# The last layer's attention in float32r halves, with its transfers merged and GpSimd's work tied to the program's order

## The chip, the cores and the metric

The kernel runs on one core of a Trainium2 chip. TensorE (PE) multiplies matrices and writes to PSUM; VectorE (DVE), ScalarE (ACT) and GpSimd (POOL) work element by element; SyncE (SP) issues the transfers, which 16 DMA engines carry out. The engines run side by side, each through its own instructions in order, and wait for each other by semaphores. The metric is device time in microseconds (us) of one execution; a time stands for the median of several.

## The reference, cut to what matters

Four layers run one after another over a state x of 4 sequences of 1024 tokens and 128 channels. The change is in the last one: attention with relative positions in 16 heads of 8 channels, times the silu of a gated feed-forward whose weights are stored as whole numbers.

```python
qx = split_head(x @ Wq.T); kx = split_head(x @ Wk.T); vx = split_head(x @ Wv.T)
ex = rel_embed[ns].reshape(n, NH, HD).transpose(1, 0, 2)
srel = srel_skew(jnp.einsum('bhnd,hmd->bhnm', qx, ex))
qk = (jnp.einsum('bhnd,bhmd->bhnm', qx, kx) + srel) * inv_dim
mask = 1000000000.0 * jnp.triu(jnp.ones((n, n), dtype=x.dtype), 1)
atten = jax.nn.softmax(qk - mask, axis=-1)
out = jnp.einsum('bhnm,bhmd->bhnd', atten, vx)   # heads joined again
s = out @ Wp.T + bp
# feed-forward, weights times 1/127
g = silu((silu(x @ wg.T) * (x @ wu.T)) @ wd.T)
x = x + s * g                                    # q, k, v and g from layernorm(x)
```

The table rel_embed has 256 rows, so distances repeat: srel_skew turns a row of 256 products per query into values by key.

## The kernel before, in words

Python code writes out every instruction; a framework then orders each engine's list by its own estimate of when operands are ready, places the tiles in memory and adds the semaphores. So the order on an engine follows the order of the code only roughly, unless an instruction is pinned with `keep_in_program_order`, which puts it behind everything written before it for its engine.

**Units.** The last layer (`layer3`, L1725) goes through 4 sequences, 4 groups i of four heads in each, and 8 tiles t of 128 queries in the order `ORDER3` = 7, 0, 6, 1, 5, 2, 4, 3: 128 units. Four heads lie at rows 0, 32, 64 and 96 of a 128-row tile, each with its 8 channels in the first 8 of its 32 rows; the other 24 rows are zero, set once (L1745). So one head's product takes 32 rows of TensorE's array, and four heads sit in it at once.

**Scores** (`scores3`, L2048). Per unit, in steps of up to 512 keys: four products of k and q into one PSUM tile of four banks, of which there is one (`"sc": 1`), L2068; then on DVE, head by head, the part beyond four tiles back (L2076) and the rest with its distances added (L2083), both with the running minimum; after the last step ACT takes the exponential (L2090). The exponentials are transposed on DVE (L1797) and weigh the values on PE (`weigh3`, L2104), two tiles of queries at a time. `finish3` (L2112) divides at the end of a group, `end3` (L2128) joins the heads at the end of a sequence and stores.

**Distances** (`relative3`, L1992). Products of q with the embeddings `emb` (L2004) for two heads and two tiles, two PSUM tiles of the three tagged "tr", copied by ACT (L2006) and written to DRAM in four transfers (L2009, L2010): 256 columns and the first 128 again, for either tile. Eight such parts belong to a group; the loop runs seven parts ahead. `shear3` (L2013) reads them back with a row step one element short, which does the skew (L2025, L2027, L2031), and GpSimd masks them (L2035). `ahead(n + 3)` calls it for the unit three further on, into two buffers for tiles 4 to 7 and one for tiles 0 to 3.

**Beside that**, one step per unit: `ffn3` (L1942) in each sequence's second group (gate and up products L1953, silu and copy on ACT L1957 and L1958, their product h on GpSimd L1959, down product L1963); `begin3` (L1903) in the third group for the next sequence: layernorm, then q and k stored to DRAM (L1927) and v (L1939). The first sequence's are made by `begin_first` (L1864) during the end of the third layer, and the weights by `prepare3` (L1676). `project3` (L1968) loads the next group's q and k, four heads' 8 rows in a transfer each (L1975); `values3` (L1979) loads v four times in pieces of 32 numbers (L1985) and copies it on GpSimd into the layout of the weighing (L1989).

The order of the work around the change is set by the loop at the end of `layer3`: per step of 512 keys the next products, a transpose, some weighing, the comparison; per unit the loads and steps named above. `step` and the lists `weighs` and `transposes` keep a unit's transposes one step behind its comparison. SP's queue carries all transfers in one order.

Of the kernel before, what the change touches and what calls it, by code (L numbers as in the profile page):

```python
# [12 lines left out]
I32 = mybir.dt.int32  # L13
AF = mybir.ActivationFunctionType
# [15 lines left out]
def _constants():  # L30
# [20 lines left out]

    parts.append(("rep8", np.where(row < 8, (col % 8) == row, 0.0)))
# [1623 lines left out]
def prepare3(k, w, W, ps):  # L1676
# [21 lines left out]
    W["emb"] = new("emb", [P, 4, 256])  # L1698
    with k.tc.tile_pool(name="pad3", bufs=1) as rp:
        pad = rp.tile([P, 2, 512], F32, tag="pad", name="pad")  # L1700
        nc.vector.memset(pad, 0.0)
        for c in range(2):
            for i in range(4):
                nc.gpsimd.tensor_copy(spread(pad[:, c, :])[:, i], heads_of(W["rel"][:, c, :])[:, i])
        for i in range(4):
            k.transpose_tiles(ps, "tr", [pad[:, c, i * P : (i + 1) * P] for c in (0, 1)], W["emb"][:, i, :])
            yield

        e0 = rp.tile([P, 4], F32, tag="e0", name="e0")
        nc.vector.tensor_copy(e0, W["emb"][:, :, 0])  # L1710
        for i in range(4):
            nc.vector.tensor_scalar(W["emb"][:, i, :], W["emb"][:, i, :], e0[:, i : i + 1], None, op0=ALU.subtract)
        nc.vector.tensor_scalar(W["emb"][:, :, 0], e0, -1.0, None, op0=ALU.mult)
        for name in ("gate", "up", "down"):
            f = rp.tile([P, 3, D], F32, tag="f" + name, name="f" + name)
# [9 lines left out]
def layer3(k, W, x3, out, eps5, ps, first):  # L1725
# [12 lines left out]
    with ExitStack() as st:  # L1738
# [3 lines left out]
        for n in range(2):  # L1742
            q, kk = p1.tile([P, 1 + T], F32, tag=f"q{n}", name="q"), p1.tile([P, T], F32, tag=f"k{n}", name="k")
            for a in (q, kk):
                (nc.gpsimd if n else nc.vector).memset(a, 0.0)  # L1745
            pairs.append((q, kk))
# [5 lines left out]
        def part(h):  # L1752

            at, h = divmod(h, 8)
            if at < 4 * NB:
                pair = ORDER3[h // 4 * 4 + h // 2 % 2] // 2
                if h % 2 == 0:
                    flats[at, pair] = dram.tile([2, 4, P, 384], F32, tag="flat", name="flat")
# [70 lines left out]
        for x, (n, first) in enumerate(tiles + [(len(units), 0)] * 4):  # L1829
# [25 lines left out]
            if pos == 6 and at + 1 < 4 * NB:  # L1855
                values = values3(k, p1, batch[(at + 1) // 4], vb, (at + 1) % 4)
                next(values)
            next(beside, None)
            ahead(n + 3)
        while weighs:  # L1860
            step()


def begin_first(k, W, pool, ps, x, eps5, first):  # L1864
# [9 lines left out]
    for n, name in enumerate(("WqT", "WkT")):  # L1874
# [6 lines left out]
        nc.sync.dma_start(out=first["qk"][n], in_=qk)  # L1881
        yield
    v = pool.tile([P, NT, D], F32, tag="ret", name="v")
    for half in range(2):
# [4 lines left out]
        nc.scalar.copy(v[:, 4 * half : 4 * half + 4], pv)  # L1889
    nc.sync.dma_start(out=first["vd"].rearrange("(t p) d -> p t d", p=P), in_=v)  # L1890
# [12 lines left out]
def begin3(k, W, p1, p2, temp, ps, dram, x3, b, eps5, seq):  # L1903
# [15 lines left out]
    seq["qk"] = dram.tile([2, P, T], F32, tag="qk", name="qk")  # L1919
    for n, name in enumerate(("WqT", "WkT")):  # L1920
# [6 lines left out]
        nc.sync.dma_start(out=seq["qk"][n], in_=qk)  # L1927
        yield
    v = temp.tile([P, NT, D], F32, tag="temp", name="v")
    for half in range(2):  # L1930
# [4 lines left out]
        nc.scalar.copy(v[:, 4 * half : 4 * half + 4], pv)  # L1935
        if half == 0:
            yield
    seq["vd"] = vd = dram.tile([T, D], F32, tag="vd", name="vd")
    nc.sync.dma_start(out=vd.rearrange("(t p) d -> p t d", p=P), in_=v)  # L1939


def ffn3(k, W, p1, temp, ps, seq):  # L1942
# [3 lines left out]
    for half in range(2):  # L1946
        tok = seq["xnT"][:, half * 512 : (half + 1) * 512].rearrange("p (t a i) -> p a t i", t=4, a=4)
        for first in (0, 2):
            h, up = (temp.tile([P, 3, 256], F32, tag="temp", name=name) for name in ("h", "up"))
            for c in range(3):  # L1950
# [8 lines left out]
                nc.gpsimd.tensor_tensor(h[:, c, :], h[:, c, :], up[:, c, :], ALU.mult)  # L1959
# [8 lines left out]
def project3(k, p2, pairs, seq, i, group):  # L1968

    nc = k.nc  # L1970
    q, kk = pairs
    group.update({"q": q, "k": kk, "sums": p2.tile([P, 4, NT], F32, tag="sums", name="sums")})
    for n, dst in ((0, q[:, 1:]), (1, kk)):
        for j in range(4):
            nc.sync.dma_start(out=dst[32 * j : 32 * j + 8], in_=seq["qk"][n, 32 * i + 8 * j : 32 * i + 8 * j + 8])  # L1975
# [3 lines left out]
def values3(k, p1, seq, vb, i):  # L1979
# [3 lines left out]
    for a in range(4):  # L1983
        rows = slice(32 * a, 32 * a + 32)
        nc.sync.dma_start(out=v[rows], in_=seq["vd"].rearrange("(n r) d -> r n d", r=32)[:, :, 32 * i : 32 * i + 32])  # L1985
    yield
    for a in range(4):
        rows = slice(32 * a, 32 * a + 32)
        nc.gpsimd.tensor_copy(vb[rows, :, :, a, :], v[rows].rearrange("p n (j d) -> p n j d", d=8))  # L1989


def relative3(k, W, temp, ps, flat, q, i, pair, jp):  # L1992
# [14 lines left out]
    rows = flat.rearrange("m j p u -> p j m u")  # L2007
    for m in range(2):
# [223 lines left out]
```

## Time and profile before

| what | us |
|---|---|
| median of 3 runs (3195.61 to 3202.51) | 3196.14 |
| the profiled execution | 3191.88 |
| its span, first to last instruction | 3190.2 |
| last layer: first loads, first score, last group's end | 2143, 2155, 3168 |
| DVE, PE, ACT, POOL busy from 2155 to 3168 | 809, 807, 632, 290 |
| share of the 16 DMA engines there | 0.70 |
| TensorE's mean granted clock there | 0.76 |

The page gives each engine's busy time, then the span in 40 slices with the busy share in tenths. A group line reads: line of the code, engine, operation, tiles written and read, shape, count, then busy time in us, mean ns of one, and the idle time of the engine ahead of it with what ended it. A line of waits reads: who waited for whom, us in all, how often, the longest. A line of the view by stretches reads: from and to, length, then busy us of PE, its weight loads, DVE, ACT and POOL with counts, granted clock, share of the DMA engines, GB/s.

The last layer's 16 groups end where the sums are inverted (L2115). Their lengths in us are, in order: 69.3, 72.5, 60.2, 64.4; 61.6, 69.6, 60.2, 58.8; 60.3, 71.1, 60.4, 60.7; 62.4, 68.9, 56.9, 55.5. The second of each four has the feed-forward beside it. "Plain" below are the third and fourth of the first three sequences, the first of the second to fourth, and the third of the last. 22.4 us follow the last group.

### The profile page before, as it was taken

To read this page: it belongs to the slowest core of one execution; us is meant where nothing else is said; L and a number is where in the kernel's file an instruction comes from. 1 tells how busy PE (TensorE), PEld (TensorE's weight loads), DVE (VectorE), ACT (ScalarE), POOL (GpSimd) and SP (SyncE) were. 2 spreads that over 40 slices of the span, in tenths; PEclk is the share of its full clock that TensorE was granted. 3 is DMA by queue.
4 is the path that set the end of the run, shared out by engine and by line. 5 is a ranking of instruction groups with operands and counts; after the bars stand their busy time and mean duration, and the time that the engine had idled before them with its cause. 6 is when DMAs were issued, how large, how long until landed. Compare 5 with 4: busy or idle time off the path is not lost. (4 is left out here: it accounts for less than half of the span.)

```text
span 3190.2 us, 50621 instructions
## 1 busy us (share of the span) xinstructions
PE 2246.5 (70%) x18321; PEld 1278.9 (40%) x18321; DVE 2302.6 (72%) x5540; ACT 1494.7 (47%) x3256; POOL 1155.6 (36%) x1086
## 2 busy tenths in 40 slices
PE   5787778577787776894443674367877877878875
PEld 2555556232333332561110222244544544545553
DVE  5555544878888886657777888656788788788786
ACT  3554544333333333525332463136665765665663
POOL 3433444144444444223477433232322322323322
PEclk9888888588878877895655566566877877877776
DMA  3000000100000000320333446328677677677772
GB/s 81 13 1 1 1 1 1 35 0 0 0 0 7 6 1 7 114 98 20 73 106 112 128 107 145 101 90 252 179 217 213 191 215 230 185 221 203 209 233 65
DMA packets 397311, 308.18 MB, mean 97 GB/s; under 512 B 96369, under 2 KB 379885, under 8 KB 391429
## 3 DMA queue, kind: packets, MB, share of 16 engines
q1 hardware_dynamic: 395908, 300.75, 32.9%
q10 hardware_dynamic: 1152, 4.19, 0.4%
q8 instruction: 144, 2.36, 0.3%
q14 instruction: 107, 0.87, 0.1%
HBM read 162.72 MB, written 141.56 MB: 95 GB/s over the span
## 5 line engine op out<-in xcount | busy, mean ns | idle before, releaser
L2090 ACT ACTIVATE neg<-neg,low 128x640 f32<-128x640 f32 (+7 forms) x512 | 390.1, 763 | 168.4 <-DVE low L2083 168.1
L2035 POOL TENSOR_SCALAR_AFFINE_SELECT rel<-rel 128x512 f32<-128x512 f32 x288 | 180.2, 637 | 625.6 <-DMA rel<-flat 459.6
L1797 DVE STREAM_TRANSPOSE wT<-neg 128x640 f32<-128x640 f32 (+7 forms) x512 | 361.7, 754 | 15.8 <-ACT neg L2090 13.4
L2068 PE MATMUL score<-k,q 32*128 32x512 f32 (+3 forms) x1536 | 276.5, 702 | 103.1 <-DVE low L2083 102.5
L2083 DVE CUSTOM_DVE_ANT_0 neg<-score,rel,low 128x128 f32<-128x128 f32 (+3 forms) x448 | 217.3, 517 | 138.2 <-issue 67.2
L2004 PE MATMUL pr<-emb,q 32*128 32x256 f32 x1024 | 227.5, 525 | 62.2 <-ACT r L2006 37.1
L2104 PE MATMUL po<-wT,vb 128*32 128x64 f32 (+1 forms) x10240 | 216.6, 241 | 44.4 <-issue 30.8
L2104 PEld LDWEIGHTS po<-wT,vb 128*32 128x32 f32 x10240 | 184.3, 128 | 144.1 <-issue 85.2
L2004 PEld LDWEIGHTS pr<-emb,q 32*128 32x128 f32 x1024 | 146.1, 249 | 136.9 <-ACT r L2006 69.1
L2006 ACT COPY r<-pr 128x512 f32<-128x512 f32 x256 | 136.4, 581 | 128.8 <-PE pr L2004 95.3
L2068 PEld LDWEIGHTS score<-k,q 32*128 32x128 f32 x1536 | 98.5, 236 | 159.8 <-DVE low L2083 115.5
L2083 DVE CUSTOM_DVE_ANT_0 neg<-score,rel 128x512 f32<-128x512 f32 (+3 forms) x320 | 149.2, 521 | 18.4 <-PE score L2068 7.2
L835 PE MATMUL pg<-xnT,w 128*128 128x512 f32 x256 | 148.1, 662 | 6.7 <-DVE h L839 3.1
L788 POOL TENSOR_TENSOR prod<-rest,kv 128x2048 f32<-128x2048 f32 x32 | 145.2, 4571 | 18.4 <-ACT rest L778 18.4
L837 PE MATMUL pu<-xin,w 128*128 128x512 f32 x256 | 141.2, 635 | 13.7 <-DVE h L839 7.6
L826 PE MATMUL po<-h,w 128*128 128x512 f32 x256 | 131.4, 635 | 26.9 <-DVE h L839 26.9
L838 ACT ACTIVATE h<-pg 128x512 f32<-128x512 f32 x128 | 75.9, 595 | 156.8 <-PE pg L835 156.7
L214 PE MATMUL pt<-ident,three 128*24 128x128 bf16 x64 | 9.2, 295 | 197.5 <-DVE three L211 197.5
L1084 PE MATMUL ph<-xin,upT 128*128 128x512 bf16 (+1 forms) x128 | 69.7, 574 | 65.2 <-DVE xin L1078 63.8
L431 PE MATMUL px<-hT,xbcT 128*128 128x512 f32 x256 | 114.7, 592 | 0.0
L1489 PE MATMUL read<-kt,const_sb 128*128 128x128 f32 x256 | 50.7, 370 | 90.3 <-POOL kt L1484 90.3
L783 DVE TENSOR_REDUCE s<-prod 128x128 f32<-128x2048 f32 x32 | 73.1, 2284 | 49.4 <-POOL prod L788 49.4
(634 smaller groups left out, 5662.8 us busy)
## 6 DMA issues: line engine op xcount, KB each, us to landing
flat<-r SPq DMA_DIRECT2D x256, 256.0 KB
rel<-flat SPq DMA_DIRECT2D x112, 512.0 KB
flat<-r SPq DMA_DIRECT2D x256, 128.0 KB
rel<-flat SPq DMA_DIRECT2D x96, 256.0 KB
kt<-kd SPq DMA_DIRECT2D x16, 512.0 KB
qt<-qd SPq DMA_DIRECT2D x16, 512.0 KB
kdc<-kdd SPq DMA_DIRECT2D x16, 512.0 KB
ktc<-ktd SPq DMA_DIRECT2D x16, 512.0 KB
```

The costliest lines, as they stand in the source:

```text
L788: nc.gpsimd.tensor_tensor(prod, attn.rearrange("p (t h g) -> p t h g", t=4, g=16)[:, t].unsqueeze(2).to_broadcast(each), kv[:, t, 1, :].re ...
L826: nc.tensor.matmul(po, W["w2"][:, e, c, :], h[:, c, :], start=(e == 0 and c == 0), stop=(e == 7 and c == 1))
L835: nc.tensor.matmul(pg, W["w1"][:, e, c * P : (c + 1) * P], xnT, start=True, stop=True)
L837: nc.tensor.matmul(pu, W["w3"][:, e, c * P : (c + 1) * P], xin, start=True, stop=True)
L1797: nc.vector.transpose(weights[at, pair][j][:, t % 2, 0 : (t + 1) * P], S[j][:, 0 : (t + 1) * P])
L2004: nc.tensor.matmul(to[:, m, :], q[at, t * P : (t + 1) * P], W["emb"][at, i, :], start=True, stop=True)
L2006: nc.scalar.copy(r[:, n], to)
L2035: nc.gpsimd.affine_select(out=rel[:, :, slot(back), :], in_=rel[:, :, slot(0), :], compare_op=op, fill=fill, base=0, pattern=[[0, 4], [-si ...
L2068: nc.tensor.matmul(sc[:, j, 0 : last - first], q[at(j), 1 + t * P : 1 + n], kk[at(j), first:last], start=True, stop=True)
L2083: nc.vector.tensor_tensor_reduce(out=neg[:, begin:last], in0=sc[:, j, begin - first : last - first], in1=rel[:, j, slot : slot + (last - b ...
L2090: nc.scalar.activation(neg[:, 0:n], neg[:, 0:n], AF.Exp, bias=here, scale=-1.0, accum_out=group["sums"][:, j, t : t + 1])
L2104: nc.tensor.matmul(o[32 * j : 32 * j + 32, 2 * pair + m.start : 2 * pair + 2, :], vb[:, kb, j].rearrange("p a d -> p (a d)"), weights[j][: ...
```

## The change

q and k become float32r tiles. Each number is split into a rounded half and the rest, and the 32 rows of a head hold four copies of its 8 channels: rounded, rounded, rest, rest for q, and rounded, rest, rounded, rest for k and the embeddings. The product over 32 rows is the sum of all four cross products. Each tensor in DRAM gets the shape in which it is read, so that q, k and v of a group come in one transfer each, and the distances of two tiles are written by two transfers in place of four. Three kinds of GpSimd work are pinned to the order of the code. The loads of distances are called for ahead of the step beside the unit.

```diff
@@ prepare3
+    W["emb"] = w.tile([P, 4, 256], F32R, tag="emb", name="emb")
...
-        nc.vector.memset(pad, 0.0)
+            for r in range(4):
+                nc.gpsimd.tensor_copy(
+                    pad[:, c, :].rearrange("p (n r d) -> p n r d", r=4, d=8)[:, :, r], W["rel"][:, c, :].rearrange("p (n d) -> p n d", d=8)
+                )
...
+            nc.vector.tensor_copy(e0, emb[:, 0:1])
+            nc.vector.tensor_scalar(emb, emb, e0, None, op0=ALU.subtract)
+            nc.vector.tensor_scalar(emb[:, 0:1], e0, -1.0, None, op0=ALU.mult)
+            nc.scalar.copy(high, emb)
+            nc.vector.tensor_tensor(emb, emb, high.bitcast(F32), ALU.subtract)
+            nc.vector.tensor_scalar(emb, emb, low, None, op0=ALU.mult)
+            nc.vector.scalar_tensor_tensor(W["emb"][:, i, :], high.bitcast(F32), top, emb, op0=ALU.mult, op1=ALU.add)
@@ layer3
-            q, kk = p1.tile([P, 1 + T], F32, tag=f"q{n}", name="q"), p1.tile([P, T], F32, tag=f"k{n}", name="k")
-            for a in (q, kk):
-                (nc.gpsimd if n else nc.vector).memset(a, 0.0)
+            q, kk = p1.tile([P, 1 + T], F32R, tag=f"q{n}", name="q"), p1.tile([P, T], F32R, tag=f"k{n}", name="k")
+            nc.vector.memset(q[:, 0:1].bitcast(F32), 0.0)
...
+            ahead(n + 3)
             next(beside, None)
-            ahead(n + 3)
@@ new, called by begin_first (by halves of 512 tokens) and begin3
+def halves3(k, n, high, a, to):
+    nc = k.nc
+    rows = to.rearrange("i j (h d) t -> h (i j) d t", h=4)
+    nc.scalar.copy(high, a)
+    for h in (0, 1 + n):
+        nc.sync.dma_start(out=rows[h], in_=high.bitcast(F32))
+    k.tc.keep_in_program_order(nc.gpsimd.tensor_tensor(a, a, high.bitcast(F32), ALU.subtract))
+    for h in (2 - n, 3):
+        nc.sync.dma_start(out=rows[h], in_=a)
+def keep_values3(nc, to, v):
+    for a in range(4):
+        nc.sync.dma_start(out=to[:, :, a], in_=v[32 * a : 32 * a + 32])
@@ begin3
-        nc.sync.dma_start(out=seq["qk"][n], in_=qk)
+        halves3(k, n, temp.tile([P, T], F32R, tag="temp", name="high"), qk, seq["qk"][n])
@@ ffn3
-                nc.gpsimd.tensor_tensor(h[:, c, :], h[:, c, :], up[:, c, :], ALU.mult)
+                k.tc.keep_in_program_order(nc.gpsimd.tensor_tensor(h[:, c, :], h[:, c, :], up[:, c, :], ALU.mult))
@@ project3
-        for j in range(4):
-            nc.sync.dma_start(out=dst[32 * j : 32 * j + 8], in_=seq["qk"][n, 32 * i + 8 * j : 32 * i + 8 * j + 8])
+        nc.sync.dma_start(out=dst.bitcast(F32), in_=seq["qk"][n, i].rearrange("j r t -> (j r) t"))
@@ values3
-    for a in range(4):
-        rows = slice(32 * a, 32 * a + 32)
-        nc.sync.dma_start(out=v[rows], in_=seq["vd"].rearrange("(n r) d -> r n d", r=32)[:, :, 32 * i : 32 * i + 32])
+    nc.sync.dma_start(out=v.rearrange("p n d -> p (n d)"), in_=bass.AP(at.tensor, at.offset, [(0, 4), (4096, 32), (1, 1024)]))
...
-        nc.gpsimd.tensor_copy(vb[rows, :, :, a, :], v[rows].rearrange("p n (j d) -> p n j d", d=8))
+        k.tc.keep_in_program_order(nc.gpsimd.tensor_copy(vb[rows, :, :, a, :], v[rows].rearrange("p n (j d) -> p n j d", d=8)))
@@ relative3, with flat of [P, 4, 2, 384] in place of [2, 4, P, 384]
-    for m in range(2):
-        nc.sync.dma_start(out=rows[:, 2 * jp : 2 * jp + 2, m, 0:256], in_=r[:, :, m])
-        nc.sync.dma_start(out=rows[:, 2 * jp : 2 * jp + 2, m, 256:384], in_=r[:, :, m, 0:P])
+    nc.sync.dma_start(out=rows[:, :, 0:256], in_=r)
+    nc.sync.dma_start(out=rows[:, :, 256:384], in_=r[:, :, 0:P])
@@ shear3
-    shear = lambda n: bass.AP(base.tensor, base.offset + t % 2 * 4 * P * 384 + P, [(383, P), (P * 384, 4), (1, n)])
+    shear = lambda n: bass.AP(base.tensor, base.offset + t % 2 * 384 + P, [(8 * 384 - 1, P), (768, 4), (1, n)])
@@ end3
-    k.update(x, s, seq["g"])
+    k.tc.keep_in_program_order(nc.gpsimd.tensor_tensor(s, s, seq["g"], ALU.mult))
+    k.tc.keep_in_program_order(nc.gpsimd.tensor_tensor(x, x, s, ALU.add))
```

## The prediction

> **What bounds the kernel now.** I first read the page's slices, to see which stage the change touches. The last layer starts at 2143 us, which is slice 27 of 40.
>
> ```profile
> PE   5787778577787776894443674367877877878875
> DVE  5555544878888886657777888656788788788786
> PEclk9888888588878877895655566566877877877776
> DMA  3000000100000000320333446328677677677772
> ```
>
> The reader is to see that no engine stands at 9 there: VectorE (DVE) and TensorE (PE) share the stage at 7 to 8 tenths, and the transfers stand at 7. So I read the busy time by stretches, cut where a group of four heads ends: a first group, two plain groups, a group with the gated feed-forward beside it, and the last group.
>
> ```profile
> core 0: us, PE busy (x) PEld busy (x) DVE busy (x) ACT busy (x) POOL busy (x), PEclk, DMA share, GB/s
> 2155.10:2224.40 69.30, 54.22 (x698) 33.47 (x697) 49.40 (x152) 43.27 (x95) 13.16 (x22) 0.66 0.85 251
> 2612.70:2671.50 58.80, 46.39 (x983) 30.30 (x985) 50.57 (x157) 37.39 (x89) 14.67 (x21) 0.83 0.84 248
> 2863.30:2924.10 60.80, 51.00 (x991) 33.39 (x988) 50.03 (x158) 37.41 (x89) 14.91 (x21) 0.75 0.81 240
> 2986.50:3055.40 68.90, 57.92 (x784) 37.23 (x786) 49.49 (x157) 49.34 (x114) 25.89 (x38) 0.85 0.67 194
> 3112.30:3167.80 55.50, 31.35 (x765) 19.16 (x753) 49.81 (x157) 25.30 (x65) 11.64 (x16) 0.63 0.25 73
> ```
>
> DVE does the same 50 us in every group; the group's length follows PE. The last group computes no distances for a successor, PE works 31 us, and the group takes 55.5. That row is my model for the changed kernel. The waits of DVE from 2155 to 3168 us say what the other groups lose:
>
> ```profile
> DVE neg L2083 <- issue: 73.0, 22, 8.0
> DVE neg L2083 <- PE score L2068: 55.9, 47, 3.9
> DVE neg L2076 <- PE score L2068: 31.7, 13, 12.7
> DVE wT L1797 <- ACT neg L2090: 13.4, 23, 1.6
> DVE neg L2083 <- POOL rel L2035: 8.8, 4, 3.8
> ```
>
> The first three are waits for scores ("issue" as well: the timeline shows PE finishing other products just before): 161 us. TensorE takes its instructions in order, one score tile is held in PSUM at a time, so a score stands behind whatever PE has ahead of it. These two groups of the page are what the change shortens:
>
> ```profile
> L2068 PE MATMUL score<-k,q 32*128 32x512 f32 (+3 forms) x1536 | 276.5, 702 | 103.1 <-DVE low L2083 102.5
> L2004 PE MATMUL pr<-emb,q 32*128 32x256 f32 x1024 | 227.5, 525 | 62.2 <-ACT r L2006 37.1
> ```
>
> **float32r.** Each float32 product is two records: 1536 for 768 scores, 1024 for 512 distances. A 512-column score tile (four products, eight records) takes 1.14 us at the full granted clock and 2.09 at half, in the timeline. No row shows float32r. Its price lies between the rows above (no gain; a loss I exclude, since the same columns are streamed over the same 32 rows) and the nearest rows of one pass, bfloat16 128x512 at L1084: 0.376 us shortest, 0.609 median. A float32r operand is a shortened one, too (the edit keeps the rest of each number in a second operand), so of the two the bfloat16 row is nearer: I take 0.5 us a tile of scores and 0.6 a part of distances (two rounds of 256 columns). 192 tiles x 0.5 = 96 in place of 276; 128 parts x 0.6 = 77 in place of 227. PE loses 330 us, 20.6 a group: a plain group falls from some 49 to 28, under the last group's 31.
>
> The granted clock may fall with it: it was 0.83 where PE was busy 46 of 58.8 us and 0.63 where it was 31 of 55.5. At half clock throughout, the remaining 28 would be 28 x 0.76 / 0.5 = 43, still under DVE's 50. So the clock alone takes nothing away in plain groups. The Trainium skill, page "TensorE: Matmul & The Clock Gate", section on the HAM clock gate, says that an idle window of about 3.4 us halves the clock; that speaks against thinning out PE. By that rule the 43 would hold everywhere, and the sum would stay, since DVE is longer.
>
> **ACT.** In the built order the table loads of the layer (exp against silu) rise from 30 to 62, because the scheduler now puts single exponentials between the feed-forward's pieces. A load takes 1.283 us in the trace: 32 x 1.283 = 41 us, all in the four groups with the feed-forward, 10 each, on an ACT that is busy 49 there. 59 of 69 us: it no longer hides. The Trainium skill, page "ScalarE: Activation LUTs", section "What ACT_TABLE_LOAD costs", stands against this reordering more strongly: at its roughly 2.7 us a load the estimate would be 86 us, 22 a group, but the measured row decides. The six rounding copies of 1024 columns (1.1 us each, as an exponential of that width) spread over three groups in which ACT has 20 us to spare.
>
> **Transfers and SP.** Writes of distances halve in number with the same bytes and the same pieces (1 KB and 512 B). The queries' and keys' loads go from 128 of 32 KB to 32 of 512 KB, their stores from one to four copies; the values' 64 loads lose their 128-byte pieces. From the trace's packets of this stage: 65,536 of 128 B at 13 ns go (54 us of 16 engines), about 7,400 of 4 KB at 202 ns come (93 us). So the DMA engines get 40 us more, 0.70 x 1012.7 = 709 becomes about 750. Against a layer of 930 us that is 0.81, which plain groups stand at today. It is hidden as long as loads stay early: the last mask of a unit (L2035) now ends 10 to 16 us (medians by tile) before DVE needs it. Fewer issues on SP (1029 rows of its order become 740, about 0.5 us each) gain nothing, as SP waits for free buffers (L2025 on DVE). Shifted loads ahead of the feed-forward step have the same cover.
>
> **GpSimd.** Ten subtractions come (1.3 us for 512 columns, 2.3 for 1024, by the sums of that shape), two memsets go: 17 us more on an engine at 289 of 1013. Pinning costs nothing in busy time. What it adds are waits: a product h (L1959) now stands behind the masks traced before it, and these behind their loads; PE's down products wait for h, and the next score is queued behind them. Now that costs 3.9 us in all. A load lands and is masked about 4 + 1.9 us after issue, h takes 2.1: 8 us, while DVE has about 10 us of work from the freed buffer (four transposes of 1024 columns 4.9, a small tile with its transposes 2.3, half a large tile 2.8). It just hides; if not, up to 8 us a step (rival 3). The subtraction's operands hold one more of three shared buffers while distances use them too: bounds 0 and 2 us for each of the six. Value copies and the final sums keep their places within a few masks: nothing, bounds -3 and +3 us a batch.
>
> **Start.** From 2095 to 2143 us DVE gets about 20 small operations for emb (0.35 each), ACT eight, POOL four subtractions, SP 17 more issues, around a chain that passes through all of them. I charge 5 us, bounds 0 and 12 (17 issues x 0.5, plus 3). The four memsets ahead of the first loads, 1 to 2 us, are in that.
>
> **The sum,** against the profiled execution (span 3190.2, 3191.9 with what lies around it; the median of the runs, 3196.1, is 4.3 above):
> - ten plain groups, 605.9 us now, to 54.5 each: the last group's 55.5, less half of its own 5.1 us of waits for scores, plus 1.5 for distances that still wait for ACT's copies (L2004 <- ACT, 37 us in all). Gain 61. Bounds 52.5 and 59 each: 81 and 16.
> - the last group 55.5 to 53: 2.5, bounds 0 and 4.
> - four feed-forward groups, 282.1 now, to 66: ACT's 59 and the waits between PE, ACT and POOL. Gain 18, bounds 62 and 75: +34 and -18.
> - the first group 69.3 to 63, since 25 us of it are distances: 6, bounds 0 and 12.
> - start -5; the tail after 3167.8 us stays.
> 82 us in all, 2.6%. On the scale of the median: **3114 us.**
>
> **Rivals.**
> 1. Everything falls to DVE's pace, the feed-forward groups too (plain 52.5, feed-forward 62): 81 + 4 + 34 + 12 - 2 = 129, about 3067. For it: the slack of the masks. Against: ACT's 59 us.
> 2. The hand-offs keep most of it: the built order puts 16 distance products in a row ahead of a score, each pair waiting for ACT to empty one of three PSUM buffers. Plain groups 58, feed-forward unchanged: 26 + 1 + 3 - 8 = 22, about 3174.
> 3. Slower: pinned products. Place: the 16 feed-forward steps. Price: up to 8 us each, the longest score wait now, 128 us, less the forecast's 82: +46, 3242. It decides from 82 / 16 = 5 us a step on, that is when loads land some 11 us after issue instead of 4 (8 us needed against 10 of cover), which a fuller DMA could do at bursts.
> 4. float32r runs no faster than float32. Then half of the 41 us of table loads and the start remain: 3196 + 25 = 3221, from 3200 to 3240.
>
> **How the numbers follow.** Forecast 57% (3085 to 3145), rival 1 14%, rival 2 16%, rival 3 7%, rival 4 6%. A difference under 0.2%, 6.4 us, can't be told from none. Faster: 57 + 14 + 15 = 86%; the same 3%, one part each of rivals 2, 3 and 4; slower 11%, the rest of 3 and 4. The range 3055 to 3175 holds the forecast and rivals 1 and 2, and leaves out 3 and 4 and little more.
>
> **What would show it.** Right: L2068 and L2004's lines together under 200 us; plain groups at 53 to 56 us with DVE at 50; 62 table loads, feed-forward groups the longest at about 66, with ACT near 59; DMA near 0.8, masks still early. Wrong: score records as long as now (rival 4); DVE's longest waits for scores behind the down products, with these waiting for POOL h, over 5 us a step (rival 3); PE's distances waiting for ACT over 100 us in all (rival 2); masks ending as DVE needs them.

## The result, and the profile after

The changed kernel takes 3200.8 us (median; 3191.6 to 3207.7), the kernel before 3196.1 (3188.5 to 3203.8). The ratio is 1.0017, with a 95% interval of 1.0009 to 1.0025: 3 to 8 us slower, where I had forecast 82 us faster. The profiled execution has a span of 3196.1 us against 3190.2.

The slices of the page, in the changed kernel:

```profile
PE   5787778577787776894443673465666666666664
DVE  5555544878888886657777888567788688687776
PEclk9888888588878878995655576566766766767666
DMA  3000000100000000320343456248688588688672
```

From slice 27 on TensorE has come down from 7 and 8 tenths to 6, and its granted clock with it. DVE stands where it stood. DMA shows 8 in every second or third slice, where 7 was the rule.

The two groups that the change was to shorten, from the same page:

```profile
L2097 PE MATMUL score<-k,q 32*128 32x512 f32 (+3 forms) x768 | 127.3, 577 | 153.4 <-DVE low L2112 153.1
L2033 PE MATMUL pr<-emb,q 32*128 32x256 f32 x512 | 129.5, 446 | 63.8 <-ACT r L2035 48.1
```

The feed-forward's down products, from the groups of instructions by line between 2155 and 3167 us:

```profile
L1993 PE MATMUL po<-downT,h 128*128 128x128 f32 x192 | 39.6, 342 | 23.2 <-POOL h L1989 23.1
```

One record per product in place of two, 257 us in place of 504: float32r does its work. A score tile of 512 columns takes 0.50 us at full clock and 0.80 at half (1.14 and 2.09 before). The products wait longer for others than they did, scores 153 us for DVE to empty the tile (102 before), down products 23 for h (4 before).

The stretches, cut where DVE first compares for the first tile of a group (columns as before: length; busy us of PE, weight loads, DVE, ACT, POOL with counts; granted clock, DMA share, GB/s). The rows are the first group, two fourth groups of a sequence, a feed-forward group, and the last group:

```profile
2155.80:2222.20 66.40, 33.02 (x429) 23.62 (x428) 44.25 (x146) 40.77 (x90) 17.21 (x25) 0.58 0.94 295
2604.00:2670.60 66.60, 42.70 (x758) 28.73 (x756) 51.79 (x159) 43.27 (x104) 18.17 (x21) 0.63 0.87 272
2860.20:2926.50 66.30, 42.55 (x758) 28.75 (x757) 51.70 (x158) 43.30 (x104) 18.17 (x21) 0.65 0.89 276
2987.20:3059.20 72.00, 49.19 (x804) 36.00 (x804) 47.82 (x155) 56.27 (x114) 24.49 (x36) 0.76 0.55 163
3118.00:3166.80 48.80, 22.56 (x684) 16.80 (x684) 46.85 (x156) 23.53 (x62) 13.45 (x19) 0.64 0.35 102
```

The last group, which has no successor, is at DVE's pace (47 of 48.8 us). The fourth groups, plain ones that I put at 54.5, take 66, with the transfers at 0.87 and 0.89. The first has them at 0.94. What DVE waited for from 2150 to 3200 us (us, times, longest):

```profile
DVE neg L2112 <- PE score L2097: 53.3, 38, 4.3
DVE neg L2112 <- issue: 47.3, 28, 3.7
DVE on L2154 <- PE pr L2152: 27.6, 12, 5.3
DVE neg L2112 <- POOL rel L2064: 26.5, 11, 12.8
DVE wT L1807 <- PE po L2133: 19.4, 7, 3.4
DVE neg L2105 <- PE score L2097: 19.2, 8, 9.8
DVE wT L1807 <- ACT neg L2119: 15.6, 21, 2.1
DVE neg L2112 <- POOL h L1989: 13.2, 3, 5.8
```

And what PE waited for in the same stretch:

```profile
PE score L2097 <- DVE low L2112: 153.1, 95, 5.5
PE po L2133 <- issue: 55.3, 29, 4.2
PE po L2133 <- DVE wT L1807: 54.5, 85, 2.8
PE pr L2033 <- ACT r L2035: 48.1, 45, 6.2
PE po L1993 <- POOL h L1989: 23.1, 10, 5.8
```

The three waits for scores (L2112, "issue", L2105) fell from 161 to 120 us. New ones fill the gap: masks 26.5 (8.8 before), PE's other products 47 (8 before), h 13 (0.5 before). So time moved from one kind of wait to others. To see it whole I took every gap between DVE's instructions, from its first comparison of the layer to its last, and asked the trace what PE was doing in it. The first four columns are the lengths of the four first, feed-forward, third and fourth groups together; then come DVE's idle time and its parts by PE's work; then, of 128 units, how many had their last mask end less than 1 us ahead of the first comparison that reads it. Times are us of one profiled execution each; the runs e1 to e17 are told below.

| kernel | first | ff | third | fourth | idle | scores | distances | weighing | other | PE idle | late masks |
|---|---|---|---|---|---|---|---|---|---|---|---|
| before | 252 | 282 | 238 | 236 | 201 | 96 | 19 | 18 | 49 | 20 | 1 |
| changed | 245 | 290 | 228 | 248 | 220 | 38 | 22 | 39 | 81 | 39 | 14 |
| e1: changed, float32 | 255 | 308 | 238 | 271 | 266 | 99 | 35 | 18 | 78 | 37 | 1 |
| e2: before, float32r halves | 265 | 294 | 241 | 278 | 276 | 45 | 27 | 47 | 76 | 81 | 36 |
| e3: changed, no pins | 245 | 275 | 236 | 245 | 212 | 38 | 20 | 43 | 61 | 49 | 10 |
| e5: before, halves | 247 | 298 | 239 | 255 | 233 | 90 | 31 | 20 | 74 | 18 | 7 |
| e12: e3, down later | 249 | 249 | 263 | 255 | 223 | 44 | 26 | 45 | 44 | 63 | 8 |
| e13: e3, fourth buffer | 259 | 302 | 237 | 241 | 251 | 34 | 32 | 43 | 76 | 66 | 5 |
| e14: e3, both | 253 | 233 | 249 | 251 | 195 | 40 | 27 | 37 | 39 | 53 | 5 |
| e15: e3, distances not through DRAM | 230 | 262 | 203 | 226 | 134 | 26 | 11 | 22 | 71 | 4 | - |
| e16: before, distances not through DRAM | 234 | 280 | 237 | 224 | 172 | 81 | 15 | 15 | 53 | 8 | - |
| e17: before, both of e14 | 247 | 263 | 248 | 235 | 189 | 95 | 17 | 26 | 30 | 21 | 2 |

The first two rows hold the result: DVE's idle time during scores fell by 58 us, and 22 came back during weighing, 32 during other products, 20 while PE was idle too, 3 during distances. That is 19 us more idle time, but from the first comparison to the last the kernel is only 3.5 us longer, since the time in which any DVE instruction runs fell from 807 to 791 us. The span grew by 5.9 us: 3.5 there and 4.6 in the tail after it, less 2.2 at the start. The ten plain groups take 605.7 us, 605.9 before.

### The profile page after: what moved, and what is told of

The parts are those of the page before. It is cut to its first block, busy times and chain, and to the rows that moved or that the text cites. A ratio compares the mean times of both kernels' runs of the same rounds, so it can differ in the third digit from the quotient of the medians.

```text
span 3196.1 us, 47596 instructions
## 1 busy us (share of the span) xinstructions
PE 2087.5 (65%) x17041; PEld 1227.6 (38%) x17041; DVE 2299.2 (72%) x5558; ACT 1541.8 (48%) x3302; POOL 1165.1 (36%) x1094
## 5 line engine op out<-in xcount | busy, mean ns | idle before, releaser
L1807 DVE STREAM_TRANSPOSE wT<-neg 128x640 f32<-128x640 f32 (+7 forms) x512 | 379.5, 764 | 35.3 <-PE po L2133 19.4
L2133 PE MATMUL po<-wT,vb 128*32 128x64 f32 (+1 forms) x10240 | 258.4, 256 | 110.0 <-issue 55.3
L2112 DVE CUSTOM_DVE_ANT_0 neg<-score,rel,low 128x128 f32<-128x128 f32 (+3 forms) x448 | 212.1, 505 | 100.2 <-PE score L2097 38.6
L2133 PEld LDWEIGHTS po<-wT,vb 128*32 128x32 f32 x10240 | 211.4, 137 | 171.1 <-issue 84.2
L2097 PE MATMUL score<-k,q 32*128 32x512 f32 (+3 forms) x768 | 127.3, 577 | 153.4 <-DVE low L2112 153.1
L2112 DVE CUSTOM_DVE_ANT_0 neg<-score,rel 128x512 f32<-128x512 f32 (+3 forms) x320 | 149.7, 521 | 48.6 <-issue 23.2
L2033 PE MATMUL pr<-emb,q 32*128 32x256 f32 x512 | 129.5, 446 | 63.8 <-ACT r L2035 48.1
L2033 PEld LDWEIGHTS pr<-emb,q 32*128 32x128 f32 x512 | 95.8, 273 | 104.4 <-ACT r L2035 66.9
L2097 PEld LDWEIGHTS score<-k,q 32*128 32x128 f32 x768 | 55.1, 240 | 206.7 <-DVE low L2112 165.8
```

The lines of the kernel that those rows point to most:

```text
L1807: nc.vector.transpose(weights[at, pair][j][:, t % 2, 0 : (t + 1) * P], S[j][:, 0 : (t + 1) * P])
L2033: nc.tensor.matmul(to[:, m, :], q[at, t * P : (t + 1) * P], W["emb"][at, i, :], start=True, stop=True)
L2097: nc.tensor.matmul(sc[:, j, 0 : last - first], q[at(j), 1 + t * P : 1 + n], kk[at(j), first:last], start=True, stop=True)
L2112: nc.vector.tensor_tensor_reduce(out=neg[:, begin:last], in0=sc[:, j, begin - first : last - first], in1=rel[:, j, slot : slot + (last - b ...
L2133: nc.tensor.matmul(o[32 * j : 32 * j + 32, 2 * pair + m.start : 2 * pair + 2, :], vb[:, kb % 4 * NT + kb // 4, j].rearrange("p a d -> p (a ...
```

## The experiments

Each was timed in turn with the kernel before on the same chip; the ratio is to that one. Costs and gains below are differences to that kernel; two runs are compared by their ratios, since the kernel before took between 3192.2 and 3196.1 us in the sessions. Theory A says that float32r pays and other parts of the change take it back; B, that the gain is lost in the alternation of PE and DVE, in the order that the framework builds; C, that the way of the distances through DRAM (queue, buffers, loads, masks) becomes the bound.

**What float32r is worth: e1, e9, e2.**

```diff
-F32R = mybir.dt.float32r
+F32R = mybir.dt.float32
```


> The whole change, but q, k and the embeddings stay float32 (the rounded half is then the number itself and the rest zero, so the same products come out); halves, transfers, GpSimd's order, table of loads as in the changed kernel. What it tells: what float32r is worth inside the changed kernel. TensorE gets back about 250 us of busy time in this layer (scores 127 to about 276, distances 130 to about 227). Theory A (TensorE's time is saved, but the rest of the change costs as much): slower than the changed kernel by the 50 to 80 us I had forecast for float32r, 3250 to 3280. Theory B (the saving is lost where it arises, because with short products the framework puts the distances and the weighing ahead of the scores, and DVE and TensorE now wait for each other): the framework's estimate of a float32 product brings back an order near that of before, so within 15 us of the changed kernel, 3185 to 3215, and DVE's waits for scores near 160 us as before.

Measured 3267.6 us, ratio 1.0227 (1.0205 to 1.0249). Float32r is worth 67 us inside the change, the other order that the framework builds from its estimate of a float32 product included, and without it the change costs 74. Theory A's number; B, as I had put it, falls.

```diff
-  nc.tensor.matmul(to[:, m, :], q[at, t * P : (t + 1) * P], W["emb"][at, i, :], ...)
+  nc.tensor.matmul(to[:, m, :], q[at, t * P : (t + 1) * P].bitcast(F32), W["emb"][at, i, :].bitcast(F32), ...)
```


> The changed kernel with the distances' products read as float32 again (512 products of two records; the operands' bits are the same), the scores in float32r. Over all of the layer DVE was idle while TensorE worked on distances for 19 us before and 22 us after, and on scores for 96 and 38. If that is what float32r is worth, the distances have no part in its 67 us: 3193 to 3210. If TensorE's whole time counts: the distances' half of the saving, 25 to 35 us, is lost: 3225 to 3240. If a busier TensorE keeps a higher granted clock and that alone shortens the rest: below the changed kernel, 3180 to 3193.

Measured 3230.7, ratio 1.0117 (1.0099 to 1.0135): 32 us slower than the changed kernel, near half of the 67. That is what was expected if PE's whole time counts, not the part that DVE's gaps show; as edits that leave PE's products alone cost 24 and 25 us too (e6, e7), this run by itself does not prove it. The granted clock did not rise (0.736 over the span, 0.738 in the changed kernel).

e2 is the kernel before with the functions for the halves (`halves3`, the float32r tiles, `emb`) and without the rest of the change; q and k are loaded so:

```diff
-  nc.sync.dma_start(out=dst[32 * j : 32 * j + 8], in_=seq["qk"][n, 32 * i + 8 * j : 32 * i + 8 * j + 8])
+  nc.sync.dma_start(out=dst[32 * j : 32 * j + 32].bitcast(F32), in_=seq["qk"][n, i, j])
```


> The kernel before with float32r halves and nothing else: no pinning, distances in four transfers, values in 128-byte pieces, loads beside as before; q and k are loaded as four transfers of 32 rows each because the halves need all 32 rows. Theory A (float32r gains, pinning, transfers or table loads take it back): 3110 to 3150. Theory B (the saving is lost in the order of the products): 3185 to 3215, score and distance records as short as in the changed kernel (about 127 and 130 us), DVE still waiting for scores over 100 us and TensorE for the transposes over 40 us.

Measured 3259.8, ratio 1.0197 (1.0177 to 1.0218): neither theory's number. Its waits of DVE:

```profile
DVE neg L2107 <- POOL rel L2059: 61.6, 26, 9.6
DVE neg L2107 <- issue: 59.1, 34, 4.2
DVE neg L2107 <- DMA rel<-flat: 54.2, 7, 10.0
```

Waits for masks and loads, 9 us before, are 116 here, with 36 late masks. This is what brought theory C: with scores out of the way, DVE runs into the distances.

**The other parts alone, in the kernel before: e5, e6, e7, e10.** e5 is e2 with `F32R = mybir.dt.float32`.

> The kernel before with the halves but in float32 (products as before, the rest halves zero): only the four-fold stores and loads of q and k, the roundings and subtractions. The kernel with float32r halves alone took 3260, 66 us over before, with DVE waiting 115 us for masks and loads. Theory C (the halves' traffic, four times the bytes of q and k in the queue that also carries the distances, makes the loads late, whatever TensorE does): 3240 to 3270, masks late as there. Theory D (additive: float32r is worth 67 us, so the halves cost 133): 3310 to 3340. Theory B (the order that the framework builds from its estimate of a float32r product makes the loads late): near before, 3195 to 3215, with masks early.

Measured 3225.4, ratio 1.0099 (1.0080 to 1.0119): +33 us. It meets none of the numbers. Float32r, worth 67 us in the change, costs 31 more here (e2 against e5). So its worth depends on what stands around it; between the two pairs the layouts in DRAM, the pins and the order of the loads differ, and these two runs do not say which of them counts.

e6 has `flat` as [P, 4, 2, 384], its two writes, `keep_values3` and the one load of values, with float32 q and k as before.

> The kernel before with the new layouts of values and distances in DRAM alone: distances written by two transfers in place of four, values stored in the order in which they are read and loaded in one transfer, without the 128-byte pieces; q and k as before. By my forecast the transfers were hidden: 3185 to 3200. If transfers are a bound of their own, as the late masks of float32r halves alone suggest: 3160 to 3185, with the idle time of DVE while TensorE is idle too falling from 20 us.

Measured 3216.1, ratio 1.0068 (1.0054 to 1.0083): +24 us, on neither side of what I expected. 17 of them lie in the first sequence's first two groups. There GpSimd once stands 10 us, with a product h next, until a load of distances lands; PE's down products wait 11 us for h, and DVE's two longest waits for a score are 13.7 and 13.4 us (6.6 and 6.1 in these groups before).

e7 pins h, the value copies and the final sums:

```diff
-  nc.gpsimd.tensor_tensor(h[:, c, :], h[:, c, :], up[:, c, :], ALU.mult)
+  k.tc.keep_in_program_order(nc.gpsimd.tensor_tensor(h[:, c, :], h[:, c, :], up[:, c, :], ALU.mult))
```


> The kernel before with GpSimd's products h, value copies and final sums pinned to the program's order, nothing else. In the changed kernel the pins cost 12 us. If they cost by themselves what they cost there: 3203 to 3210, the groups with the feed-forward some 10 to 15 us longer in all and TensorE's down products waiting for h over 15 us. If they cost only where scores are short: within 5 us of before, 3190 to 3199.

Measured 3217.0, ratio 1.0065 (1.0047 to 1.0083): +25 us, more than either number. The feed-forward groups are 12 us longer in all, and down products wait 14 us for h (4 before).

```diff
-  next(beside, None)
   ahead(n + 3)
+  next(beside, None)
```


> The kernel before with the loads of distances called ahead of the step beside the unit, nothing else: the last part not yet tried alone. The other parts alone, without float32r, cost 33 (halves), 24 (transfers) and 25 us (pins), all together 74. If the sum holds: -10 to 0, 3182 to 3193. If any disturbance of the order in which before was built costs its 20 to 30 us, whatever it is meant to do: 3205 to 3225.

Measured 3195.2, ratio 1.0007 (0.9998 to 1.0016): +2 us. So not every disturbance of the order costs 20. The four parts together make 84 us; all of them at once (e1) cost 74.

**The pins and the order inside the change: e3, e8, e4, e11.** e3 takes `keep_in_program_order` away in all four places.

> The changed kernel with GpSimd's four kinds of instructions free to be ordered by the framework again. If pinning takes the gain back (rival 3 of the prediction: products h behind the masks): 3120 to 3150, and TensorE's down products wait for h under 8 us in all in place of 23. If the order on TensorE does: within 10 us of the changed kernel, 3190 to 3210.

Measured 3189.1, ratio 0.9986 (0.9974 to 0.9998), by the ratios 10 us under the changed kernel. Down products wait 11 us for h in place of 23, the feed-forward groups fall from 290 to 275. The pins take 10, then, not the bulk.

```diff
+  next(beside, None)
   ahead(n + 3)
-  next(beside, None)
```


> The changed kernel with the step beside the unit called ahead of the loads of distances again, as before the change. In my forecast the order of these two has no price: within 5 us of the changed kernel, 3193 to 3207. If the pinned products h wait because the masks, and their loads, now stand ahead of them, this brings back what pinning cost: 3185 to 3192, and TensorE's waits for h fall from 23 us to under 10. If the loads need the lead, masks late as in float32r halves alone: 3215 to 3260.

Measured 3190.7, ratio 0.9997 (0.9986 to 1.0007): 6 us under the changed kernel, and the wait for h falls to 11 as well. With e3 it says the same: h stood behind masks and their loads, and these 6 to 10 us were it.

e4 passes every instruction that the last layer gives to `nc.tensor` through `keep_in_program_order`.

> The changed kernel with all TensorE instructions of the last layer in the order of the code: the products of the next score step first, then transposes and weighing, as the loop is written. Theory B (the framework's order on TensorE eats the saving): DVE's waits for scores fall from 160 us to under 90 and TensorE's wait for the transposes from 54 to under 30, 3120 to 3160. Theory A, or that the hand-offs through PSUM set the pace whatever the order: 3190 to 3230; slower still if the code's order, which was never used as such, puts products ahead of data that come late.

Measured 3228.9, ratio 1.0099 (1.0080 to 1.0119), slower: PE now waits 352 us for the score tile. e11 gives scores priority, on e3:

```diff
+  with k.tc.high_priority():
       for j in range(4):
           nc.tensor.matmul(sc[:, j, 0 : last - first], ...)
```


> The changed kernel without the pins, and the scores' products traced with high priority, so that the framework puts them on TensorE as soon as it thinks the tile free. If scores stand late because other products were put ahead of them (theory B): DVE's waits for scores fall from 77 us to under 40, 3150 to 3180. If the hand-over itself sets the pace (one tile of scores, which DVE must empty before TensorE fills it), no order helps: 3180 to 3200, or slower, where the products that are put behind come late for the weighing.

Measured 3197.3, ratio 1.0007 (0.9996 to 1.0018). DVE's idle time during scores falls from 38 to 33 us and that of both engines rises from 49 to 57. Neither of these two orders of PE's products brings anything, which speaks against theory B; other orders were not tried.

**The way of the distances: e15, e16.** In `relative3` the two writes go, `shear3` goes, and the units read one zero tile:

```diff
-  rels[n] = shear3(k, p2 if t > 3 else p1, flats[n // 8, t // 2], t)
+  rels[n] = still[t > 3]
```


> The changed kernel without the pins, and without the way of the distances through DRAM: their products and copies stay, the writes, loads and masks are left out, and the comparisons read one still tile of zeros. So DVE, TensorE and ACT do all their work, and nothing of it waits for a load or a mask. If late loads and masks keep the gain (theory C): 3090 to 3130. If TensorE and DVE wait for each other as they did before, only with shorter products (theory B): 3165 to 3190.

Measured 3110.8, ratio 0.9743 (0.9728 to 0.9758): 78 us under e3, in the range of theory C.

> The kernel before with the same left out. Its masks were 10 to 16 us early and DVE waited 9 us for them, so little should go: 3170 to 3192. The difference between this one and the one before it in this list is what float32r and the halves are worth where no transfer of distances is in the way: by the 67 us measured with transfers and the halves' 33, 35 us or so; by my forecast over 80.

Measured 3164.7, ratio 0.9913 (0.9897 to 0.9929): 28 us under before, a little more than I expected. So the change without its pins gains 54 us where the distances are out of the way, between the 35 and the 80 that I had named, and the way of the distances costs 50 us more in e3 (78) than in the kernel before (28). DVE's waits in e3 say where most of that stands:

```profile
DVE neg L2112 <- POOL rel L2064: 37.6, 12, 11.2
DVE neg L2112 <- POOL h L1989: 17.4, 5, 8.8
```

With 2 us for another instruction of GpSimd's, DVE waits 57 us for that engine, as far as the profile names the semaphore that came last; before it is 9, and in e15 and e16 it is nothing. e15's second sequence, the feed-forward group and the two after it:

```profile
2444.60:2510.50 65.90, 47.55 (x804) 35.88 (x804) 50.02 (x159) 51.53 (x117) 11.96 (x15) 0.76 0.08 27
2510.50:2561.10 50.60, 31.27 (x727) 21.82 (x724) 49.13 (x174) 37.77 (x90) 4.13 (x4) 0.63 0.10 23
2561.10:2620.50 59.40, 39.74 (x754) 26.96 (x754) 51.07 (x158) 41.34 (x96) 8.87 (x6) 0.64 0.41 130
```

A third group takes 50.6 us with DVE busy for 49.1, at a granted clock of 0.63. That is the pace that I had forecast for all plain groups and a little better. In a third group PE, its clock and ACT allow it; what keeps the real kernel from it there is the way of the distances. The first groups of the later sequences and the fourth ones stay at 58 to 60 us even here, so the ten plain groups take 557, not the 545 of my sum.

How that comes about can be followed in a fourth group of the changed kernel. SP's queue, from the timeline (start, length, engine, line):

```profile
2622.88 1.17 SPq L1880 DMA_DIRECT2D qk<-high  x2
2625.37 2.20 SPq L1883 DMA_DIRECT2D qk<-qk  x2
2627.61 1.45 SPq L2038 DMA_DIRECT2D flat<-r  x1
2629.10 1.81 SPq L2039 DMA_DIRECT2D flat<-r  x1
2631.01 1.14 SPq L2054 DMA_DIRECT2D rel<-flat  x1
```

And ACT in the same stretch (in brackets the idle time before, and what ended it):

```profile
2629.65 0.59 ACT L1965 COPY v<-pv 128x512 f32<-128x512 f32 x1 [4.42 <-DMA qk<-high]
```

The load for the unit t = 1 stands on SP behind four stores of k's halves and two writes, 8 us in all. Its mask ends at 2637.3, 0.8 us ahead of the comparison. Meanwhile ACT's copy of v waits 4.4 us until a store has left one of the three shared buffers, and with it the distances' copies behind it. Here DVE does not wait for the mask. It waits 2.8 us for exponentials that stand behind the copies of v on ACT, most of it in this row:

```profile
2634.05 1.11 DVE L1807 STREAM_TRANSPOSE wT<-neg 128x896 f32<-128x896 f32 x1 [1.64 <-ACT neg L2119]
```

From the first comparison to the last, ACT's waits for transfers make 58 us in the changed kernel, 16 before and under 1 in e15.

**Two edits that help: e12, e13, e14, e17, e18.** On e3:

```diff
+  yield
   po = ps.tile([P, 2, D], F32, tag="tr", name="po")
```


> The changed kernel without the pins, and the feed-forward's down products called one unit after the gate, up and h that they need, so that none of them waits for h on its engine. In the four groups with the feed-forward DVE is idle for 82 us (98 with the pins), 42 (60) of them while TensorE works on products other than scores, distances and weighing. If the wait for h makes these: these groups lose 15 to 25 us together, 3165 to 3178. If it is the products' own time ahead of a score, the waits stay and only move: 3182 to 3196. The h that is kept over a unit holds one of three shared buffers: if that counts, slower, up to 3215.

Measured 3199.2, ratio 1.0023 (1.0014 to 1.0032). The feed-forward groups fell by 25 us, as expected if the wait for h made them, though ACT's table loads there also fell, from 14 to 10 in a group; the third groups rose by 27.

```diff
-  p1, p2, temp, dram = pool("l3", 1), pool("l3d", 2), pool("l3r", 3), ...
+  p1, p2, temp, dram = pool("l3", 1), pool("l3d", 2), pool("l3r", 4), ...
-  by_t = p2.tile([P, 8, 32], F32, tag="by_t", name="by_t")
+  by_t = temp.tile([P, 8, 32], F32, tag="temp", name="by_t")
```


> The changed kernel without the pins, and the shared buffers of 4 KB (distances, h, up, the halves and their source, x and its layernorm) four in place of three; the 1 KB of the inverted sums' spread move into one of them to make room. ACT's copies of distances wait some 18 us, its other copies 25 us, for a transfer to leave such a buffer, and these stand ahead of writes and loads on the queue. If distances come late for want of buffers (theory C): 3160 to 3180. If TensorE's chain of products and DVE is the bound: 3184 to 3192.

Measured 3225.7, ratio 1.0107 (1.0089 to 1.0125): 39 us slower than e3, which neither theory has. 27 of them are in the feed-forward groups, where down products wait 32 us for h (11 in e3), 14 in the first groups. Late masks fell from 10 to 5. Why a spare buffer makes the built order put h later was not tried.

> The same fourth buffer in the kernel that calls the down products a unit later. There the groups with the feed-forward fell by 25 us, as expected, but the groups after them rose by 27, with masks coming late and ACT's copies waiting 4 us at a time for a buffer. If the buffers carried the loss from one group into the next: 3165 to 3180. If something else is the bound and only moves the loss about (TensorE's products at the lower clock, the queue): 3190 to 3205.

Measured 3172.5, ratio 0.9937 (0.9921 to 0.9952): faster than both kernels. With the down products later, the fourth buffer gains 27 us (e12), with the feed-forward groups 16 us shorter and the third ones 13. A feed-forward group:

```profile
2469.70:2527.10 57.40, 41.34 (x772) 30.67 (x772) 46.79 (x154) 44.27 (x93) 21.53 (x31) 0.76 0.74 226
```

> The kernel before with the down products a unit later and the fourth shared buffer, the two edits with which the changed kernel without its pins took 3172 and beat both. It tells whose merit that is. If the two edits help any kernel: 3165 to 3180 here too, and the change has given nothing even there. If they take away what the change brought with it (waits for h, buffers held by the halves): 3185 to 3205 here. If the ffn's groups are held by float32 scores instead: their 282 us stay.

Measured 3168.0, ratio 0.9919 (0.9906 to 0.9931). The two edits gain 25 us without any of the change. The 20 us of e14 are theirs, and the change brings nothing in that structure either (3172 against 3168).

```diff
-  if pos == 3 and i == 2 and b + 1 < NB:
+  if pos == 0 and i == 2 and b + 1 < NB:
```


> The kernel with later down products, a fourth buffer and no pins (3172), with the step that makes the next sequence's q, k and v called from the third group's first unit on in place of its fourth. It then ends in that group, not in the fourth, where in the changed kernel stores of the halves held the shared buffers (ACT's copy waited 4.4 us for one, the loads behind it came late) and which took 251 us where 226 were reached without the way of the distances. If that chain is what lengthens the fourth groups (theory C): these fall by 10 to 20 us, and the whole to 3152 to 3165. If the loss only moves into the third groups, as that of the feed-forward did once: 3167 to 3178.

Measured 3179.7, ratio 0.9956 (0.9943 to 0.9969), on e14. The fourth groups fell from 251 to 230 us, so the step that makes the next sequence's q, k and v, halves among them, is what lengthens them; the third rose from 249 to 269. The loss moves with the step. How much of it is the halves' this run does not say: the step was not moved in the kernel before.

## Why the prediction was wrong, point by point

- **float32r: the mechanism right, the size too large.** 0.50 us a score tile was right at full clock, but of the 96 tiles of 512 columns 63 ran at half clock (38 before): the scores took 127 us, not 96, the distances 130, not 77. PE lost 162 us between 2155 and 3167, not 330: the granted clock there fell from 0.76 to 0.68, and weighing alone (L2133) went from 214 to 251 us. A plain group keeps PE busy for 35 to 43 us, not 28. The worth of 67 us is what e1 shows.
- **The clock.** That it takes nothing away in plain groups holds in e15's third groups (50.6 us at 0.63). The Trainium skill, page "TensorE: Matmul & The Clock Gate", section on the HAM clock gate, says that idle windows lower the clock; the granted 0.68 goes that way, but that the clock bounds a group no run here shows, nor how much of the 22 us of idle time that came back during weighing is its doing.
- **ACT's table loads.** The count, 62 for exp and silu, and ACT's 56 us in the feed-forward groups (forecast 59) were right, the conclusion is not shown. ACT stands idle for 16 of the 72 us of such a group, and in e3 the last three of these groups have the same 14 loads each and are 3 to 5 us shorter, with the waits for h down. So h, which was not in this term, had a part in their length. e14, with groups of 58 us and 63 loads from 2150 us on (65 in the changed kernel), does not decide it, since only 8 or 9 loads fall into each of its feed-forward groups. The Trainium skill's roughly 2.7 us a load (page "ScalarE: Activation LUTs", section "What ACT_TABLE_LOAD costs") would by an estimate have added 20 us more to each group with 14 loads; every load in the traces takes 1.283 us.
- **Transfers and SP: the step that failed.** "It is hidden as long as loads stay early." The sizes were right (0.74 of the 16 engines against 0.70, 40 us of 1012). But I measured the cover, 10 to 16 us, in a kernel whose scores were slow, and took it over into one whose scores are not: there it is 4.5 to 11 (medians by tile), and late masks went from 1 to 14. From a unit's last load to its first mask the median went from 3.8 to 4.9 us. In e1, with the same transfers and slow scores, it is 3.8 and one mask is late. "Fewer issues on SP gain nothing" missed that one issue gets longer: 0.50 us in the mean before, 0.71 after (979 issues in 493 us, 619 in 441, from 2155 to 3150); part of that is their size, but loads of unchanged size went from 0.51 to 0.74. The price is 50 us, 78 (e15 under e3) less 28 (e16 under before).
- **GpSimd: "It just hides."** It did not: 10 us (e3), 25 by itself (e7). The place was rival 3's, the price 0.6 us a step and not 8.
- **The halves' steps.** I put 0 to 2 us on each of six subtractions for a shared buffer. Alone the halves cost 33 us (e5), all of it in feed-forward and fourth groups; e18 moves 21 us with the step that makes them.
- **Start and tail.** The first comparison came 2 us earlier, not 5 later. Without float32r it came 15 later (e1), and 16 later with the distances alone in float32 (e9), so short first distances made up for the rest of the start; the halves alone cost 2 (e5). The tail, which I had unchanged, took 29.3 us in place of 24.7, counted from the last comparison. It takes back the 3.4 us by which the last group, my model, got shorter; e1, with float32, has 52.2 and 24.3 us as before.
- **Groups.** The ten plain ones, forecast at 545, took 606, as before: the third ones gained 10 us together, the first ones of the later sequences 5, and the fourth ones of the first three lost 15. The feed-forward groups took 290 us (264 forecast), the first 66 (63), the last 49 (52 before by this cut; my 53 stood against 55.5, up to the inversion).
- **The rivals.** Rival 2 said that hand-offs keep most of it, by distances waiting for ACT; that wait is 48 us, far from the 100 that I named. Rival 4 is out, by the records. None of them was the case that came: float32r gains 67 us inside the change, and parts that I had priced at nothing or little take all of it. My 3114 is close to e15's 3111, but that is luck: e15 leaves out GpSimd's masks and some 460 of SP's issues too, which is worth 28 us in the kernel before as well (e16). Against e16 the gain is 54 us, not 82. So the 87 us between forecast and result are about 28 by which the sum was too high even with the distances out of the way, 50 for their way through DRAM, and 10 for the pins.

Open: how the 50 us divide between SP's queue, the shared buffers, the transfers themselves and the masks on GpSimd, all of which e15 leaves out or relieves together; and why single edits, e13 above all, make the built order lose 20 to 40 us. Every part "alone" contains its own built order, so the 33, 24 and 25 us, and the 67 of float32r, are prices in that kernel and not constants; e15 and e16 are built in orders of their own as well, so the 50 us are known no better than to some 20.

## What to carry to other kernels

Slack that hides a transfer belongs to the pace at which it was measured: whoever shortens the bound must put the same loads, waits and buffers against the new pace, part by part, before calling them hidden. Let the best case be tested by leaving the suspected way out (e15), in both kernels: it shows in two runs what the speed-up could bring and what stands against it. And a version that beats both kernels proves nothing for the change until its extra edits have been tried without it (e17).

## What the runs showed of the hardware

One product in float32r over 32 rows leaves one record, float32 two; four of 512 columns side by side take 0.50 us at the full granted clock and 0.80 at half, float32 1.14 and 2.09. SP's issue of the same 206 loads of distances took 104 us before, 152 in the changed kernel: 0.51 and 0.74 us each, though their sizes did not change. In e1, with all of the change but float32r, they took 0.55.
